# Constants of square roots as numbers, norm scaling on GpSimd, and one add of a block from VectorE to ScalarE

## The chip, the core and the metric

The kernel runs on one core of a Trainium2 chip, all in float32. The core's engines work side by side, each through its own instructions in order: TensorE (PE in the profile, with PEld for its weight loads), VectorE (DVE), ScalarE (ACT), GpSimd (POOL) and SyncE (SP), which here only issues DMAs. They wait for each other through semaphores. The metric is the device time of one execution in microseconds (us), the median of several runs.

## What is computed

Two transformer layers over x of 4 x 1024 x 256. Each layer normalizes, attends, adds, normalizes, applies a feed-forward part and adds. The first layer's attention is a recurrent state (RWKV) and its feed-forward part a mixture of experts; the second layer is the pair attention below with a ternary feed-forward network. The second layer takes three quarters of the time and holds the main part of the change. Cut to it:

```python
def _rho_signed_sqrt(x):
    return jnp.sqrt(jax.nn.relu(x) + EPS_RHO) - jnp.sqrt(jax.nn.relu(-x) + EPS_RHO)
q = jnp.einsum('bnc,ac->bna', X, Wq)                # X: 4 x 1024 x 256, 64 channels a
k = jnp.einsum('bnc,ac->bna', X, Wk)
Vy = jnp.einsum('bnc,dc->bnd', X, Wy_w) + Wy_b
e = jax.nn.relu(_rho_signed_sqrt(q[:, :, None, :] + k[:, None, :, :]))
scores = jnp.einsum('bija,a->bij', e, Wphi)
ex = jnp.exp(scores - jnp.max(scores, axis=-1, keepdims=True))
denom = jnp.sum(ex, axis=-1)
part1 = jnp.einsum('bij,bjc->bic', ex, Vy)
Ew = jnp.einsum('bij,bija->bia', ex, e)
part2 = jnp.einsum('bia,ca->bic', Ew, We_w) + We_b * denom[..., None]
return (part1 + part2) / (denom[..., None] + EPS_DEN)
```

For every pair of a query i and a key j and each of 64 channels, a root of relu(q + k) + eps has to be made: 268 million roots. A layer norm is (x - mean) / sqrt(var + eps), followed by a scale and a shift per channel.

## The kernel before

**The first layer** (`first_layer`) runs over units of 512 tokens. Its roots are in `normed` (L328) and in `outputs` (L516), with eps read from a tile. Its own `normed` scales on DVE (L334) and is not touched otherwise.

**The second layer** (`pair_attention`) works in 128 blocks of 32 queries against 1024 keys. A block has 32 queries x 64 channels x 1024 keys of roots to make. Its queries and channels are spread over the 128 partitions, so that the block consists of 16 operations of 128 x 1024, numbered i = 0 to 15, held in 8 tiles "s" of two each (a pair p has i = 2p and 2p + 1). Each pair goes through this:

- `begin(p)`: for those i which the table ADDS gives to POOL ("p"), POOL adds the query's column to the keys (L1399), then clamps between 0 and the largest number (L1404), over one half or both halves of the tile.
- `adds(p)`: for those that ADDS gives to DVE ("d"), DVE adds and takes the maximum with 0 (L1413).
- `pair(p)`: for those that ADDS gives to ACT ("a"), ACT does a relu with the query as its bias (L1424). Then ACT takes the root of the whole tile of 128 x 2048 (L1425), and PE makes 8 products (16 records in the trace) that sum the scores in `sc` (L1429).
- `weigh(p, h, ew)`: DVE multiplies the tile's half with the exponentials in `xb` and sums (L1475). This frees the tile.

Between them stand, once for a block: `top` (DVE's maximum over the scores, L1439, L1441, and a product on PE, L1442), `exps` (DVE's L1446, then ACT's exponential L1448, and behind it the silu or gelu of the dense part, L1372, through `switch`), `spread` (PE's copy of the exponentials into `xb`, L1455) and `turn`.

The tiles "s" are a ring of 14 (RING). The main loop goes over blocks n and turns p = 0 to 7. In turn p it emits the weighing of pair p of block n, the DVE add of the pair that ACT will take next, at p = 5 `top` and at p = 6 `exps` of the next block, then `work(ROOM[p])`, and then `begin` and `make` of later pairs, 14 ahead for `begin` and two less for `make`. All queues are in the order of emission, written out by hand. Before the change ADDS reads

```python
ADDS = ('ap', 'pp', 'pp', 'dp', 'pp', 'ap', 'dp', 'ap')
```

so that pairs 0, 5 and 7 have their first add on ACT, pairs 3 and 6 on DVE, and the other 11 of 16 are POOL's. In block 0 the rule is another: ACT has i < 6 and DVE the rest.

**Work between the turns.** `work(room)` steps generators. `tasks` holds `finish`, the output of four blocks; `stream` holds the larger parts in order: `first_rest` (the first layer's last unit), `prepare(b)` (queries, keys and values of the next batch, started at block 12 of a batch of 32) and `dense(j)`, the feed-forward network for 256 tokens, of which there are 16, one for each eight blocks. A generator yields the number of its products, until a turn's room is used up; a yield without a number ends the stream's turn. So a turn of PE carries the scores of one pair and up to six dense products.

**The second layer's `normed`** (L917 to L952) is a generator too, called 16 times with n = 2 tiles from `head` (the start of a `dense`), 6 times with n = 4 from `prepare` and once from `first_rest`: 23 calls and 60 tiles of 128 x 256. DVE makes the statistics (L925, L926), ACT the root (L928), DVE after a yield the reciprocal (L930). For two tiles at a time DVE then scales (L937), PE transposes (L941) and, after another yield, ACT applies scale and shift (L944). The scaled tiles `ln_xn` have two buffers.

Of the kernel before, what the change touches and what calls it, by code (L numbers as in the profile page):

```python
# [31 lines left out]
PREP = 12  # L32
ROOM = (4, 6, 6, 6, 6, 4, 3, 6)
LATE = 2
ADDS = ('ap', 'pp', 'pp', 'dp', 'pp', 'ap', 'dp', 'ap')
FIRST_ON_SCALAR = 6
LEAD = 2
FLT_MAX = 3.4028234e38
# [5 lines left out]
@with_exitstack  # L44
def block_kernel(ctx: ExitStack, tc: tile.TileContext, a, out):
    nc = tc.nc
    keep = ctx.enter_context(tc.tile_pool(name="keep", bufs=1))


    kept = ctx.enter_context(tc.tile_pool(name="kept", bufs=1, space=DRAM))  # L50
    link = {
        "x1": [kept.tile([U, C], F32, tag=f"x1_{j}", name=f"x1_{j}") for j in range(B * T // U)],
        "x2": [kept.tile([FB, C], F32, tag=f"x2_{j}", name=f"x2_{j}") for j in range(B * T // FB)],
        "gates": [kept.tile([1, 2, B, C], F32, tag=f"gates{j}", name=f"gates{j}") for j in range(2)],
        "brow": kept.tile([1, C], F32, tag="brow", name="brow"),
        "yg": kept.tile([P, 4, U], F32, tag="yg", name="yg"),
        "qd": kept.tile([T, 64], F32, tag="qd0", name="qd0"),
        "nd": kept.tile([64, T], F32, tag="nd0", name="nd0"),
        "kd": kept.tile([8, P, T], F32, tag="kd0", name="kd0"),
        "vd": kept.tile([T, C + 1], F32, tag="vd0", name="vd0"),  # L60
    }

    ident = keep.tile([P, P], F32, tag="ident", name="ident")
    nc.scalar.dma_start(ident, a["ident"])
    eps = keep.tile([P, 3], F32, tag="eps", name="eps")
    for i, v in enumerate((EPS_LN, EPS_GN, EPS_RHO)):
        nc.vector.memset(eps[:, i : i + 1], v)
    cols = [keep.tile([P, 6, 2, B], F32, tag=f"mcols{i}", name=f"mcols{i}") for i in range(2)]
    seen = keep.tile([P, NE], F32, tag="seen", name="seen")
    link["qt"] = [keep.tile([P, 64, 8], F32, tag=f"qt{i}", name=f"qt{i}") for i in range(2)]  # L70
    link["wsel"] = [keep.tile([P, n], F32, tag=f"wsel{n}", name=f"wsel{n}") for n in (16, 8)]
    nc.gpsimd.memset(seen, 0.0)
    first_layer(tc, a, link, cols, seen, ident, eps)
    pair_attention(tc, a, link, out, cols, seen, ident, eps)


class Router:
# [73 lines left out]
    nc.sync.dma_start(qt[16 * i : 16 * i + 16], qd.rearrange("(m i) n -> i m n", i=16)[:, :, 8 * i : 8 * i + 8])  # L151


def first_layer(tc, a, link, cols_of, seen, ident, eps):

# [13 lines left out]

    nc = tc.nc
    NJ = 2 * HN
    eps_ln, eps_gn = eps[:, 0:1], eps[:, 1:2]
    cols = cols_of[0]
    with tc.tile_pool(name="fl_x", bufs=1) as xp, tc.tile_pool(name="fl_w", bufs=1) as wp, tc.tile_pool(
        name="fl_wd", bufs=2
# [141 lines left out]
        def normed(u, first, dest, cols=cols):  # L319

            b, xu = u * U // T, rows_of_x(u)
            st = p1.tile([P, UT, 6], F32, tag="ln_st", name="ln_st")
            mv = p1.tile([P, UT, 2], F32, tag="ln_mv", name="ln_mv")
            for i in range(UT):
                nc.vector.bn_stats(st[:, i, :], xu[:, i, :])
                nc.vector.bn_aggr(mv[:, i, :], st[:, i, :])
            rs = p1.tile([P, UT], F32, tag="ln_rs", name="ln_rs")
            nc.scalar.activation(rs, mv[:, :, 1], AF.Sqrt, bias=eps_ln)  # L328
            yield
            nc.vector.reciprocal(rs, rs)  # L330

            def scaled(t):
                xn = p2.tile([P, C], F32, tag="ln_xn", name="ln_xn")
                nc.vector.tensor_scalar(xn, xu[:, t, :], mv[:, t, 0:1], rs[:, t : t + 1], ALU.subtract, ALU.mult)  # L334
                return xn

            xs = [scaled(0), scaled(1)]
            yield
            for hf in range(2):
                ps = misc([P, 2, 2 * P], "ln_ps")  # L340
                for i in range(2):
                    xn = xs.pop(0)
                    for cc in range(2):
                        nc.tensor.transpose(ps[:, cc, i * P : (i + 1) * P], xn[:, cc * P : (cc + 1) * P], ident)
                    del xn
                    if not hf:
                        xs.append(scaled(2 + i))
                yield
                for cc in range(2):
                    nc.scalar.activation(  # L350
                        dest[:, cc, 2 * hf * P : 2 * (hf + 1) * P],
                        ps[:, cc, :],
                        AF.Identity,
                        bias=cols[:, first, cc, b : b + 1],
                        scale=cols[:, first + 1, cc, b : b + 1],
                    )
                del ps
# [139 lines left out]
        def outputs(u):  # L497

            while summed.get(u, 0) < 2:
                yield  # L500
            b, xu = u * U // T, rows_of_x(u)
            y, gat = ready[u].pop("v"), ready[u].pop("g")
            ready.pop(u)
            sq = p1.tile([P, 2, U], F32, tag="wide", name="sq")
            for cc in range(2):
                ps = misc([P, U], "cen_ps")
                nc.tensor.matmul(ps, center, y[:, cc, :], start=True, stop=True)
                yield
                nc.scalar.activation(sq[:, cc, :], ps, AF.Square)
                nc.scalar.copy(y[:, cc, :], ps)  # L510
                del ps
            for cc in range(2):
                ps = misc([P, U], "var_ps")
                nc.tensor.matmul(ps, avg, sq[:, cc, :], start=True, stop=True)
                yield
                nc.scalar.activation(sq[:, cc, :], ps, AF.Sqrt, bias=eps_gn)  # L516
                del ps
            for cc in range(2):
                nc.vector.reciprocal(sq[:, cc, :], sq[:, cc, :])
                yield  # L520
                yc, g = y[:, cc, :], gat[:, cc, :]
                nc.vector.scalar_tensor_tensor(yc, yc, chan[:, cc, CH_LW : CH_LW + 1], sq[:, cc, :], ALU.mult, ALU.mult)
                nc.vector.scalar_tensor_tensor(g, yc, chan[:, cc, CH_LB : CH_LB + 1], g, ALU.add, ALU.mult)
            yield
            for t in range(0, UT, 2):
                ps = misc([P, 2, C], "wo_ps")
                for i in range(2):
                    for cc in range(2):
                        nc.tensor.matmul(
                            ps[:, i, :], gat[:, cc, (t + i) * P : (t + i + 1) * P], wm["o"][:, cc, :], start=cc == 0, stop=cc == 1  # L530
                        )
                yield
                tmp = p1.tile([P, 2, C], F32, tag="res", name="res")
                nc.vector.tensor_tensor(tmp, ps, rows[:, 0, b : b + 1, :].to_broadcast([P, 2, C]), ALU.mult)
                del ps
                nc.gpsimd.tensor_add(xu[:, t : t + 2, :], xu[:, t : t + 2, :], tmp)
                del tmp
# [298 lines left out]
        finished(moe)  # L836


def pair_attention(tc, a, link, out, cols_of, seen, ident, eps):

# [7 lines left out]
    nc = tc.nc  # L850
    NB = T // 32
    cols = cols_of[1]
    eps_ln, eps_gn, eps_rho = (eps[:, i : i + 1] for i in range(3))
    src, dst = link["x1"], link["x2"]
    with tc.tile_pool(name="at_k", bufs=1) as pk, tc.tile_pool(name="at_w", bufs=1) as wp, tc.tile_pool(
        name="at_2", bufs=2
# [63 lines left out]
        def normed(xl, n, b, first, hT, cols=cols):  # L920
# [3 lines left out]
            for i in range(n):  # L924
                nc.vector.bn_stats(st[:, i, :], xl[:, i, :])  # L925
                nc.vector.bn_aggr(mv[:, i, :], st[:, i, :])  # L926
            rs = p2.tile([P, n], F32, tag="ln_rs", name="ln_rs")
            nc.scalar.activation(rs, mv[:, :, 1], AF.Sqrt, bias=eps_ln)  # L928
            yield
            nc.vector.reciprocal(rs, rs)  # L930
            for i in range(0, n, 2):
                while not banks[0]:
                    yield
                ps = bank([P, 2, 2 * P], "ln_ps")
                for j in range(2):
                    xn = p2.tile([P, C], F32, tag="ln_xn", name="ln_xn")
                    nc.vector.tensor_scalar(  # L937
                        xn, xl[:, i + j, :], mv[:, i + j, 0:1], rs[:, i + j : i + j + 1], ALU.subtract, ALU.mult
                    )
                    for cc in range(2):  # L940
                        nc.tensor.transpose(ps[:, cc, j * P : (j + 1) * P], xn[:, cc * P : (cc + 1) * P], ident)  # L941
                yield
                for cc in range(2):
                    nc.scalar.activation(  # L944
# [123 lines left out]
        def first_rest():  # L1068
# [37 lines left out]
            for cc in range(2):  # L1106
# [3 lines left out]
                nc.tensor.matmul(ps, avg, flat[:, cc, :], start=True, stop=True)  # L1110
                yield 2
                yield
                nc.scalar.activation(flat[:, cc, :], ps, AF.Sqrt, bias=eps_gn)
                del ps
                banks[0] += 1
            yield
# [261 lines left out]
        class Block:  # L1378
# [38 lines left out]
            def pair(self, p):  # L1417
# [3 lines left out]
                for h in range(2):  # L1421
                    i = 2 * p + h
                    if self.on_scalar(i):
                        nc.scalar.activation(t[:, h, :], kB[self.b][i % 8], AF.Relu, bias=self.query(i))  # L1424
                nc.scalar.activation(t, t, AF.Sqrt, bias=eps_rho)  # L1425
                for h in range(2):
                    g = (2 * p + h) % 8
                    for j in range(4):
# [315 lines left out]
```

## Time and profile before

The time before is 4841.81 us, the median of 3 runs (4838.57 to 4844.68). The profiled execution took 4842.18 us, its span is 4840.4 us; the granted clock of TensorE was 0.916 of full speed on average.

| Line | Engine | Operation | Count | Mean ns |
|---|---|---|---|---|
| L1475 | DVE | weigh half a tile | 2048 | 1212 |
| L1399 | POOL | add, 128 x 1024 | 1397 | 1151 |
| L1404 | POOL | clamp, 128 x 2048 | 381 | 1927 |
| L1404 | POOL | clamp, 128 x 1024 | 635 | 1092 |
| L1429 | PE | score products (records) | 16384 | 412 |
| L1330 | PE | dense products (records) | 4096 | 394 |
| L928 | ACT | root of a norm's variance | 23 | about 300 |

The table is read so: line and engine name a group of like instructions of kernel.py, "mean ns" is one instruction's duration. Matmuls overlap each other, so that their durations can't be added. The profile also tells which work ended each wait ("x <- y: us in total, times, longest us") and a chain of waits: from the last instruction back to what released it, and so on, which gives each line's share of the path that set the end.

### The profile page before, as it was taken

The numbers are of one execution on the slowest core, as the hardware profiler recorded it, in microseconds if no ns is written. First come the engines' busy times: TensorE is split into PE (matmuls) and PEld (weight loads), VectorE is DVE, ScalarE is ACT, GpSimd is POOL, SyncE is SP. The second block draws the span as 40 slices with busy tenths as digits, with TensorE's granted clock in tenths as the row PEclk, the third lists the DMA queues.
The fourth block names the chain that finished last, engine by engine and source line by source line (L and its number), as shares of the span: only waits on it lengthen the run. The fifth ranks groups of instructions, "written<-read, shape, count | busy, mean of one in ns | idle before, by whom it ended". The sixth has DMA issues, their size and how long they took to land.

```text
span 4840.4 us, 76605 instructions
## 1 busy us (share of the span) xinstructions
PE 4247.3 (88%) x28714; PEld 2421.3 (50%) x28714; DVE 3925.3 (81%) x6874; ACT 3411.3 (70%) x3182; POOL 3545.5 (73%) x2882
## 2 busy tenths in 40 slices
PE   6899999986889788989898989888899899898888
PEld 1233333432346455656554655555455556555567
DVE  5899999868897787888887787888877878888871
ACT  2333333228888888888987887888888888988851
POOL 3544444337898788888987888898878988989840
PEclk8799999987899898999998999999899989999899
DMA  4344333441112232312122332212132322122223
GB/s 139 91 119 118 107 111 110 129 137 34 42 62 72 78 98 73 125 56 90 64 73 84 102 110 75 89 64 77 54 112 94 106 72 90 64 75 76 77 85 116
DMA packets 255955, 429.48 MB, mean 89 GB/s; under 512 B 71784, under 2 KB 142624, under 8 KB 255328
## 3 DMA queue, kind: packets, MB, share of 16 engines
q1 hardware_dynamic: 252512, 422.09, 27.7%
q8 instruction: 226, 3.70, 0.3%
q10 hardware_dynamic: 2880, 1.98, 0.1%
q14 instruction: 145, 1.19, 0.1%
q0 software_dynamic: 192, 0.52, 0.0%
HBM read 400.32 MB, written 40.93 MB: 91 GB/s over the span
## 4 chain that ended last, share of the span: by engine, by line
PE 59%; ACT 15%; DVE 13%; issue 7%; POOL 5%; DMA 1%; SPq 0%; ACTq 0%; POOLq 0%; DVEq 0%
PE ff_ps L1330 16%; PE sc L1429 13%; ACT s L1425 7%; PE e_ps L620 7%; DVE s L1475 4%; PE ff_ps L1260 4%; PE xb L1455 3%; POOL s L1399 3%; POOL s L1404 2%; PE out_ps L1351 2%; PE o L1526 2%; DVE state L813 2%; PE proj_ps L425 2%; PE mix_ps L405 1%; ACT s L1424 1%
## 5 line engine op out<-in xcount | busy, mean ns | idle before, releaser
L1475 DVE CUSTOM_DVE_ANT_0 s<-s,xb 128x1024 f32<-128x1024 f32 x2048 | 2394.0, 1212 | 60.5 <-PE xb L1455 48.4
L1425 ACT ACTIVATE s<-s,eps 128x2048 f32<-128x2048 f32 x1024 | 2019.2, 1999 | 125.9 <-POOL s L1404 64.7
L1399 POOL TENSOR_SCALAR s<-kB,qt 128x1024 f32<-128x1024 f32 x1397 | 1599.7, 1151 | 321.7 <-DVE ew L1475 129.7
L1404 POOL TENSOR_SCALAR s<-s 128x1024 f32<-128x1024 f32 x1016 | 1427.4, 1405 | 89.1
L1429 PE MATMUL sc<-s,wsel 128*32 128x256 f32 x16384 | 1170.2, 412 | 329.4 <-ACT s L1425 328.7
L1330 PE MATMUL ff_ps<-wide,fw 128*128 128x256 f32 x4096 | 1001.8, 394 | 24.3 <-ACT wide L1372 21.1
L1429 PEld LDWEIGHTS sc<-s,wsel 128*32 128x32 f32 x16384 | 459.1, 115 | 900.1 <-ACT s L1425 482.2
L1330 PEld LDWEIGHTS ff_ps<-wide,fw 128*128 128x128 f32 x4096 | 762.5, 193 | 231.0 <-issue 102.2
L745 POOL TENSOR_TENSOR kv<-vb,out_k 128x512 f32<-128x512 f32 x256 | 323.7, 1273 | 242.9 <-DVE state L813 163.1
L1424 ACT ACTIVATE s<-kB,qt 128x1024 f32<-128x1024 f32 x387 | 439.5, 1136 | 18.2 <-DVE acc L603 17.5
L620 PE MATMUL e_ps<-wd,hid 128*128 128x512 f32 x896 | 414.6, 609 | 7.0 <-DVE acc L603 4.3
L1455 PE MATMUL xb<-ex,pick 64*128 64x256 f32 x2048 | 317.3, 432 | 46.2 <-ACT ex L1448 45.9
L813 DVE TENSOR_TENSOR_SCAN state<-dec,carry,kv 128x512 f32<-128x512 f32 x256 | 326.1, 1274 | 25.3 <-ACT dec L800 19.6
L620 PEld LDWEIGHTS e_ps<-wd,hid 128*128 128x128 f32 x896 | 169.7, 195 | 231.0 <-issue 216.9
L1413 DVE TENSOR_SCALAR s<-kB,qt 128x1024 f32<-128x1024 f32 x264 | 283.6, 1076 | 0.3 <-issue 0.3
L1455 PEld LDWEIGHTS xb<-ex,pick 64*128 64x128 f32 x2048 | 191.1, 201 | 178.9 <-ACT ex L1448 78.4
L1260 PE MATMUL ff_ps<-wide,fw 128*128 128x256 f32 x1024 | 269.9, 413 | 6.2 <-ACT wide L944 5.8
L805 ACT COPY carry<-state 128x1 f32<-128x1 f32 x255 | 47.9, 188 | 300.3 <-DVE state L813 299.8
L1439 DVE TENSOR_REDUCE sc<-sc 128x1 f32<-128x256 f32 x128 | 55.0, 430 | 243.7 <-PE sc L1429 243.6
L1314 DVE TENSOR_TENSOR wide<-ff_ps,ffn_s 128x512 f32<-128x512 f32 x128 | 87.9, 687 | 195.0 <-PE ff_ps L1330 194.6
L1260 PEld LDWEIGHTS ff_ps<-wide,fw 128*128 128x128 f32 x1024 | 200.3, 205 | 66.2 <-issue 20.6
L1448 ACT ACTIVATE ex<-sc,neg 128x256 f32<-128x256 f32 x128 | 60.7, 474 | 227.0 <-DVE neg L1446 226.3
(254 smaller groups left out, 4168.9 us busy)
## 6 DMA issues: line engine op xcount, KB each, us to landing
fw<-in_ffw_dram SPq DMA_DIRECT2D x354, 512.0 KB
vb<-vd SPq DMA_DIRECT2D x1024, 64.0 KB
lent<-vd SPq DMA_DIRECT2D x64, 514.0 KB
wd<-in_w_down_dram SPq DMA_DIRECT2D x28, 1024.0 KB
kB<-kd SPq DMA_DIRECT2D x32, 512.0 KB
lent<-in_We_dram SPq DMA_DIRECT2D x32, 512.0 KB
kd<-nd SPq DMA_DIRECT2D x24, 512.0 KB
vd<-out_v SPq DMA_DIRECT2D x8, 512.0 KB
```

Source lines behind the costliest of these rows:

```text
L620: nc.tensor.matmul(ps, hid[:, k, t * P : (t + 1) * P], wd[:, k, :], start=k == 0, stop=k == HID // P - 1)
L745: nc.gpsimd.tensor_mul(kv, vb[:, g % 2, :], ready[u]["k"][:, n // HN, :])
L813: nc.vector.tensor_tensor_scan(s[:, 1 : U + 1], dec, kv, c, ALU.mult, ALU.add)
L1260: nc.tensor.matmul(ps[:, h, :], w[:, k, o : o + P], hT[:, k, :], start=k == 0, stop=k == 1)
L1330: nc.tensor.matmul(ps[:, h, :], w[:, k * P : (k + 1) * P], of[:, k, :], start=k == 0, stop=k == 7)
L1399: nc.gpsimd.tensor_scalar(self.s[p][:, h, :], kB[self.b][i % 8], 1.0, self.query(i), ALU.mult, ALU.add)
L1404: nc.gpsimd.tensor_scalar(both, both, FLT_MAX, 0.0, ALU.min, ALU.max)
L1424: nc.scalar.activation(t[:, h, :], kB[self.b][i % 8], AF.Relu, bias=self.query(i))
L1425: nc.scalar.activation(t, t, AF.Sqrt, bias=eps_rho)
L1429: nc.tensor.matmul(self.sc[32 * j : 32 * j + 32, 0:256], wsel[:, g, 16 * (1 - s) : 16 * (1 - s) + 32], t[:, h, 256 * j : 256 * (j + 1)], s ...
L1455: nc.tensor.matmul(xb[:, 256 * j : 256 * (j + 1)], pick[q, j % 2, s, :], self.ex[q, :], start=True, stop=True)
L1475: nc.vector.tensor_tensor_reduce(t[:, h, :], t[:, h, :], self.xb[s], 1.0, 0.0, ALU.mult, ALU.add, ew[:, self.n % 4, col : col + 1])
```

## The change

Three edits. The roots get their eps as a number in the instruction, and the tile of constants goes. The second layer's `normed` flips the sign of the means on DVE, scales on POOL (add, then multiply) before it asks for a bank of PSUM, and yields twice between scaling and transposes. Pair 6 has its first add on ACT in place of DVE. (Parameters `eps` dropped from calls are left out.)

```diff
-ADDS = ('ap', 'pp', 'pp', 'dp', 'pp', 'ap', 'dp', 'ap')
+ADDS = ('ap', 'pp', 'pp', 'dp', 'pp', 'ap', 'ap', 'ap')
...
-    eps = keep.tile([P, 3], F32, tag="eps", name="eps")
-    for i, v in enumerate((EPS_LN, EPS_GN, EPS_RHO)):
-        nc.vector.memset(eps[:, i : i + 1], v)
...
-            nc.scalar.activation(rs, mv[:, :, 1], AF.Sqrt, bias=eps_ln)
+            nc.scalar.activation(rs, mv[:, :, 1], AF.Sqrt, bias=EPS_LN)
...
-                nc.scalar.activation(sq[:, cc, :], ps, AF.Sqrt, bias=eps_gn)
+                nc.scalar.activation(sq[:, cc, :], ps, AF.Sqrt, bias=EPS_GN)
...
                 nc.vector.bn_aggr(mv[:, i, :], st[:, i, :])
+            nc.vector.tensor_scalar_mul(mv[:, :, 0], mv[:, :, 0], -1.0)
             rs = p2.tile([P, n], F32, tag="ln_rs", name="ln_rs")
-            nc.scalar.activation(rs, mv[:, :, 1], AF.Sqrt, bias=eps_ln)
+            nc.scalar.activation(rs, mv[:, :, 1], AF.Sqrt, bias=EPS_LN)
             yield
             nc.vector.reciprocal(rs, rs)
             for i in range(0, n, 2):
+                xs = []
+                for j in range(2):
+                    xn = p2.tile([P, C], F32, tag="ln_xn", name="ln_xn")
+                    nc.gpsimd.tensor_scalar(
+                        xn, xl[:, i + j, :], mv[:, i + j, 0:1], rs[:, i + j : i + j + 1], ALU.add, ALU.mult
+                    )
+                    xs.append(xn)
+                del xn
+                yield
+                yield
                 while not banks[0]:
                     yield
                 ps = bank([P, 2, 2 * P], "ln_ps")
                 for j in range(2):
-                    xn = p2.tile([P, C], F32, tag="ln_xn", name="ln_xn")
-                    nc.vector.tensor_scalar(
-                        xn, xl[:, i + j, :], mv[:, i + j, 0:1], rs[:, i + j : i + j + 1], ALU.subtract, ALU.mult
-                    )
                     for cc in range(2):
-                        nc.tensor.transpose(ps[:, cc, j * P : (j + 1) * P], xn[:, cc * P : (cc + 1) * P], ident)
+                        nc.tensor.transpose(ps[:, cc, j * P : (j + 1) * P], xs[j][:, cc * P : (cc + 1) * P], ident)
+                del xs
                 yield
...
-                nc.scalar.activation(t, t, AF.Sqrt, bias=eps_rho)
+                nc.scalar.activation(t, t, AF.Sqrt, bias=EPS_RHO)
```

## The prediction

> **What bounds the kernel now.** I read the engines' busy times first, then the stretches, the chain of waits, the groups of instructions by line, and last the timeline. The three kinds of work lie one after the other: a first layer until 1102.6 us, the 128 blocks of pair attention until 4697.6 us, and 143 us in which only the last dense products are left. Columns of a stretch: its bounds, its length, then busy us and instructions of PE, PEld, DVE, ACT and POOL; the clock and the DMA come last.
>
> ```profile
> 1102.60:4697.60 3595.00, 3143.19 (x25380) 1923.31 (x25377) 2999.71 (x5406) 3064.70 (x2256) 3064.71 (x2461) 0.91 0.24 79
> 4697.60:4840.40 142.80, 124.25 (x541) 106.31 (x540) 18.58 (x36) 14.46 (x15) 3.25 (x3) 0.94 0.34 113
> 4048.50:4264.50 216.00, 193.00 (x1600) 121.20 (x1596) 183.67 (x331) 190.97 (x139) 193.66 (x156) 0.93 0.23 74
> ```
>
> The third line is one round of eight blocks, which recurs every 216 us. No engine is the bound alone: PE is busy 89% of the round, POOL 90%, ACT 88%, DVE 85%. What a change of 3% in one engine is worth must then be read from the chain of waits over the block stage, with the share that each line has of the path:
>
> ```profile
> by line: PE ff_ps L1330 21.9%; PE sc L1429 17.7%; ACT s L1425 9.6%; DVE s L1475 5.5%; issue 5.5%; PE ff_ps L1260 4.8%; PE xb L1455 4.5%; POOL s L1399 3.7%; POOL s L1404 2.9%; PE out_ps L1351 2.6%; PE o L1526 2.5%; ACT s L1424 1.9%; ACT L142
> ```
>
> PE's named lines alone are 54% of it. What ACT, DVE and POOL gain counts only in the rest, and there they take turns, because they wait for each other in a ring:
>
> ```profile
> PE sc L1429 <- ACT s L1425: 328.7, 204, 8.1
> DVE sc L1439 <- PE sc L1429: 243.6, 79, 10.5
> ACT ex L1448 <- DVE neg L1446: 226.3, 70, 9.2
> POOL s L1399 <- DVE ew L1475: 129.7, 128, 5.1
> ```
>
> PE's score products wait for ACT's root, DVE's maximum (L1439) for the products, ACT's exponential for that maximum, and POOL's next add for a tile that DVE frees.
>
> **The change, part by part.** These groups price it (busy us, mean ns):
>
> ```profile
> L1425 ACT ACTIVATE s<-s,eps 128x2048 f32<-128x2048 f32 x1024 | 2019.2, 1999 | 125.9 <-POOL s L1404 64.7 <-DVE s L1413 22.3 <-ACT s L1424 1.5
> L1372 ACT ACTIVATE wide<-wide 128x2048 f32<-128x2048 f32 x32 | 61.1, 1911 | 67.3 <-DVE wide L1314 66.9
> L1424 ACT ACTIVATE s<-kB,qt 128x1024 f32<-128x1024 f32 x387 | 439.5, 1136 | 18.2 <-DVE acc L603 17.5
> L1413 DVE TENSOR_SCALAR s<-kB,qt 128x1024 f32<-128x1024 f32 x264 | 283.6, 1076 | 0.3 <-issue 0.3
> L937 DVE TENSOR_SCALAR ln_xn<-wide,ln_mv,ln_rs 128x256 f32<-128x256 f32 x28 | 26.6, 988 | 0.5
> L937 DVE TENSOR_SCALAR ln_xn<-res,ln_mv,ln_rs 128x256 f32<-128x256 f32 x32 | 32.1, 1044 | 0.6
> L334 DVE TENSOR_SCALAR ln_xn<-x,ln_mv,ln_rs 128x256 f32<-128x256 f32 x68 | 31.7, 504 | 3.0 <-PE ln_ps L344 2.3
> ```
>
> *Constants.* The roots at L1425 read eps from a tile; the activations at L1372, of the same size, read none and take 88 ns less. 1024 x 0.088 = 90 us off ACT. On the path L1425 has 9.6% of 3595 = 345 us, 173 roots: 173 x 0.088 = -15 us. Ends: 0 (the number is still fetched like a tile) and -90 (every root on the path). I take -15, because the changed program's order of instructions lists the root with its data as sole input and no memset for the constants. The few small roots of the norms and the first layer (44 more) weigh under 4 us and are left at nothing: ACT is idle 70% of the first layer's time.
>
> *Pair 6 from DVE to ACT.* ACT gets 127 adds more (block 0 has its own rule): 127 x 1.136 = +144 us, so that ACT is up 54 us net. The present adds at L1424 have 1.9% of 3595 = 68 us on the path, 15.5% of their 439.5; the new ones at that share: +22 us. Ends: 0 and +144. DVE loses 127 x 1.076 = 137 us. Its main line L1475 has 5.5% of 3595 = 198 us on the path, 8.3% of 2394: -11 us. Ends 0 and -137. The pair's root now waits for no DVE; that wait was only 22.3 us for both pairs.
>
> *Norms.* 60 scalings leave DVE: 26.6 + 32.1 = 59 us. In the stretch of a preparing norm, 2550 to 2600 us, the eight of them took 7.9 us, and of the path in that stretch L937 had 5.6% of 50 us = 2.8 us, 35% of them:
>
> ```profile
> by line: ACT s L1425 15.8%; DMA wide<-x 14.2%; DVE s L1475 13.8%; PE sc L1429 11.5%; PE q_ps L985 7.2%; ACT s L1424 6.3%; DVE ln_xn L937 5.6%; DVE ln_st L925 5.4%; issue 4.2%; ACT wide L944 3.2%; DVE ln_mv L926 2.9%; ACT ewt L1495 2.7%; PE
> ```
>
> So 59 x 0.35 = -21 us; ends 0 and -59. POOL gets 60 of a form that the trace doesn't have there. Below: the clamp L1404 takes 1041 ns for 1024 elements and 1894 for 2048 at their fastest, so 256 would take 0.40 us. Above: the add of two tensors of 128x256 at L1550, 0.734 us. I take 0.55, since two per-partition operands come on top (L1399 with one takes 81 ns more than L1404 at the fastest): 33 us. L1399 and L1404 have 6.6% of 3595 = 237 us on the path, 7.8% of their 3027: +3 us. A sign flip on DVE, 23 x 0.16 us (the small operations at L930), adds 1 us at most. Norms together: -17 us.
>
> *The wait that comes with it.* On POOL the scaling stands in order before the next L1399 and waits for DVE's reciprocal (L930). Behind it queue the adds that ACT's roots need. POOL's adds waited behind that reciprocal already 16.2 us in 9 cases, 1.8 us each. 23 norms x 1.8 = 41 us at the upper end, of which 7.8% on the path, 3 us, if POOL is then as little on the path as now; I take 0, since DVE itself stood at the reciprocal then and the ring held POOL back anyway.
>
> *Collisions.* DVE's one-input operations and POOL's delay each other. Columns: start, us, engine, line.
>
> ```profile
> 3006.71 0.75 DVE L1413 TENSOR_SCALAR s<-kB,qt 128x1024 f32<-128x1024 f32 x1
> 3014.08 1.04 POOL L1404 TENSOR_SCALAR s<-s 128x1024 f32<-128x1024 f32 x1
> 3014.23 1.44 DVE L1413 TENSOR_SCALAR s<-kB,qt 128x1024 f32<-128x1024 f32 x1
> 3015.22 1.44 POOL L1399 TENSOR_SCALAR s<-kB,qt 128x1024 f32<-128x1024 f32 x1
> ```
>
> With POOL idle DVE's add takes 0.75 us; begun during a POOL operation it ends 0.69 us later, and POOL's next takes 1.44 where 1.12 is its floor. Over the floors L1399 and L1404 lose 77 us in all. About half goes with pair 6 and the norms: 38 x 7.8% = -3 us. End: -38.
>
> *Order.* Two added yields per pair of tiles make a norm two turns longer. In the order of PE's instructions the dense products lag by up to 92 of 2816 after a preparation, catch up before each next one, and 30 more (276 for 246) stand behind the last scores. A dense product (two records in the trace) takes 0.466 us there (22.39 us for 96 records): +14 us in the tail, and -14 x 0.59 = -8 in the blocks, by PE's share of the whole run's chain: +6 us. Ends: -8 and +14.
>
> ```profile
> PE 59%; ACT 15%; DVE 13%; issue 7%; POOL 5%; DMA 1%; SPq 0%; ACTq 0%; POOLq 0%; DVEq 0%
> ```
>
> **Sum**: -15 + 22 - 11 - 17 - 3 + 6 = -18 us. The profiled execution took 4842.18 us, of which 4840.4 is the span; the median of the runs is 4841.81, so 4842 serves for both: **4824 us**.
>
> **Two rules that speak against the change.** The Trainium skill (ScalarE: Activation LUTs, Rules for kernel authors) says that adds and relus belong on VectorE. VectorE: DVE Perf Modes (the section on the TRN2 errata) would price DVE's add in its two-fold mode at (58 + 512)/0.96 = 0.59 us, an estimate; 127 of these are worth 75 us and the DVE term 6 instead of 11: 4829. The row says 1.08, and 0.75 undisturbed. The GPSIMD Engine Reference (Engine selection) keeps elementwise work on VectorE. The first layer's L334 shows why, 0.40 us at its fastest; with 60 x 0.40 = 24 us saved at 35% the sum would be 4837. But beside a busy POOL the row is 1.0 us, and I go by the row.
>
> **Rivals.** *ACT becomes the bound* (slower). Pairs 5, 6, 7 and 0 then make ACT do add and root four times in a row between two exponentials, just before DVE's maximum needs pair 7. Its price is the 54 us net; it decides once ACT holds over half of the path outside PE. With 60% of ACT's terms counting (-54 + 86), no DVE gain, norms -10, order and collisions +3: 4867. For it: ACT idles only 25 us of a 216 us round. Against: 226 us of its idle time is one wait, for L1446, after these pairs. *PE holds everything* (no change): every gain outside PE's part is met by a PE wait, and only norms at -10 and order at +6 remain: 4838. For it: PE's 89%. Against: PE waited 328.7 us for roots. *DVE counts for more* than its chain share: POOL's waits for tiles are DVE's lateness, and a ring of four waits shows only its last link. With 30% of 137 + 59 us, ACT's +7, +3: 4793. *POOL's new wait on the path*: +41 us on the forecast, 4865.
>
> **How the numbers follow.** A measurement of this kernel tells about 0.2%, 9.7 us, from no change. Forecast 0.40 and DVE for more 0.12: faster 0.52. PE holds: same 0.18. ACT bound 0.22 and POOL's wait 0.08: slower 0.30. The forecast alone spans 4800 to 4848, from its terms' halves and doubles; for 8 in 10 the range takes in most of the rivals of both signs, 4782 to 4868.
>
> **What would show it.** Roots at 1.91 us; L1413 at half its count and nearer 0.75; no DVE scaling beside POOL, and POOL's at 0.4 to 0.73 us; ACT up by some 54 us, DVE down by 190, POOL within 20; the wait of DVE's maximum for scores no longer than 244 us; the tail 14 us longer. Wrong if ACT's share of the chain grows by more than 3 points, if POOL waits for L930's successor more than 60 us, or if the round of eight blocks is not shorter than 216 us.

## The result, and the profile after

The changed kernel takes 4865.40 us (median of 6 runs, 4861.63 to 4867.41) where the kernel before takes 4839.57 us beside it (6 runs): a ratio of 1.0049, with a 95% interval of 1.0039 to 1.0059. It is slower by 26 us (24 against the median of the time before), where the forecast was 18 us faster. The profiled execution took 4862.24 us, 4860.5 of it the span. The lines of the changed kernel stand three lower: L1425 is now L1428, L1424 is L1427, L1413 is L1416, L1399 is L1402, L1404 is L1407; the norm's scaling is L931.

First the busy times, and then the groups by line (count, busy us, mean ns, idle time ahead of them and what ended it), of the kernel after:

```profile
PE 4258.4 (88%) x28714; PEld 2425.3 (50%) x28714; DVE 3757.6 (77%) x6707; ACT 3455.7 (71%) x3310; POOL 3533.0 (73%) x2942
```

```profile
L1428 ACT ACTIVATE s<-s 128x2048 f32<-128x2048 f32 x1024 | 1925.2, 1907 | 115.0 <-POOL s L1407 52.6 <-DVE s L1416 13.5 <-POOL s L1402 0.7
L1427 ACT ACTIVATE s<-kB,qt 128x1024 f32<-128x1024 f32 x514 | 585.3, 1139 | 18.3 <-DVE acc L599 17.5
L1416 DVE TENSOR_SCALAR s<-kB,qt 128x1024 f32<-128x1024 f32 x137 | 143.3, 1049 | 0.0
L1402 POOL TENSOR_SCALAR s<-kB,qt 128x1024 f32<-128x1024 f32 x1397 | 1582.6, 1139 | 313.8 <-DVE ew L1478 112.5 <-PE sc L1432 60.7 <-DVE neg L1449 34.1
L931 POOL TENSOR_SCALAR ln_xn<-res,ln_mv,ln_rs 128x256 f32<-128x256 f32 x32 | 17.6, 556 | 23.2 <-DVE ln_rs L926 11.2 <-PE sc L1432 10.4 <-issue 1.6
```

Each edit did what the diff says, at the prices foreseen. The root fell from 1999 to 1907 ns. ACT has 127 adds more at 1139 ns, DVE 127 less, and POOL scales a tile in 556 ns. Only DVE's remaining adds got hardly cheaper: 1049 ns after 1076, not nearer 750. So prices of instructions are not where the forecast failed; the waits are:

```profile
PE sc L1432 <- ACT s L1428: 354.9, 219, 7.2
DVE sc L1442 <- PE sc L1432: 313.3, 89, 9.5
DVE wide L1317 <- PE ff_ps L1333: 250.5, 59, 12.2
ACT ex L1451 <- DVE neg L1449: 208.4, 60, 6.5
```

PE waits 26 us longer for roots than before (328.7), although each root is 92 ns shorter. DVE's maximum waits 70 us longer for score products (243.6), and DVE's dense steps wait 56 us longer for PE (194.6 us at L1314 before). Selected lines of the timeline, start and length in us, show the first two at work (in brackets the idle time ahead of an operation and what ended it):

```profile
4411.91 0.43 DVE L1442 TENSOR_REDUCE sc<-sc 128x1 f32<-128x256 f32 x1 [2.27 <-PE sc L1432]
...
4427.92 1.15 ACT L1427 ACTIVATE s<-kB,qt 128x1024 f32<-128x1024 f32 x1
...
4429.16 1.92 ACT L1428 ACTIVATE s<-s 128x2048 f32<-128x2048 f32 x1
4430.99 1.13 ACT L1427 ACTIVATE s<-kB,qt 128x1024 f32<-128x1024 f32 x1
4432.21 1.91 ACT L1428 ACTIVATE s<-s 128x2048 f32<-128x2048 f32 x1
4434.02 1.14 ACT L1427 ACTIVATE s<-kB,qt 128x1024 f32<-128x1024 f32 x1
4434.17 1.07 PE L1432 MATMUL sc<-s,wsel 128*32 128x256 f32 x16 [1.97 <-ACT s L1428]
4435.25 1.91 ACT L1428 ACTIVATE s<-s 128x2048 f32<-128x2048 f32 x1
4436.73 0.43 DVE L1442 TENSOR_REDUCE sc<-sc 128x1 f32<-128x256 f32 x1
4437.21 1.93 PE L1432 MATMUL sc<-s,wsel 128*32 128x256 f32 x16 [1.97 <-ACT s L1428]
```

ACT does add, root, add, root almost without a gap, one pair in about 3.05 us, and PE twice stands 1.97 us idle for a root. DVE's maximum at 4411.91 stood 2.27 us idle for score products. The next one, at 4436.73, didn't wait: DVE was weighing up to it. The chain of waits of this profile can't be used: it breaks off at POOL's scaling with a single unexplained gap.

By stretches, the pair attention starts at 1105.4 us (1102.6 before), and 173.5 us remain behind the last block's maximum (168.7 before). The rest of the loss is inside the blocks. Eight blocks near the end (112 to 119), with the same 1596 weight loads in both, are the clearest; the first line is of before, the second of after (bounds, length, busy us and instructions of PE, PEld, DVE, ACT, POOL):

```profile
4264.50:4480.70 216.20, 191.43 (x1600) 119.98 (x1596) 182.99 (x331) 190.80 (x139) 193.35 (x156) 0.94 0.22 74
```

```profile
4271.90:4495.00 223.10, 196.78 (x1600) 122.13 (x1596) 174.44 (x321) 194.06 (x146) 192.02 (x158) 0.92 0.22 72
```

The same products take 6.9 us longer, and no engine is fuller in share of the time: ACT was busy 88% and is now 87%, POOL 89% and 86%. An engine that had become the bound of these blocks would show the opposite, so that load alone doesn't explain them. PE is busy 5.35 us longer with the same products, at a granted clock of 0.92 for 0.94 (the number third from the end); by an estimate, if all of PE's time goes with the clock, 191.43 x 0.94 / 0.92 - 191.43 = 4.2 us of it come from there.

### The profile page after: what moved, and what is told of

The parts are those of the page before. It is cut to its first block, busy times and chain, and to the rows that moved or that the text cites. A ratio compares the mean times of both kernels' runs of the same rounds, so it can differ in the third digit from the quotient of the medians.

```text
span 4860.5 us, 76632 instructions
## 1 busy us (share of the span) xinstructions
PE 4258.4 (88%) x28714; PEld 2425.3 (50%) x28714; DVE 3757.6 (77%) x6707; ACT 3455.7 (71%) x3310; POOL 3533.0 (73%) x2942
## 5 line engine op out<-in xcount | busy, mean ns | idle before, releaser
L1428 ACT ACTIVATE s<-s 128x2048 f32<-128x2048 f32 x1024 | 1925.2, 1907 | 115.0 <-POOL s L1407 52.6
L1402 POOL TENSOR_SCALAR s<-kB,qt 128x1024 f32<-128x1024 f32 x1397 | 1582.6, 1139 | 313.8 <-DVE ew L1478 112.5
L1407 POOL TENSOR_SCALAR s<-s 128x1024 f32<-128x1024 f32 x1016 | 1400.1, 1378 | 89.0
L1427 ACT ACTIVATE s<-kB,qt 128x1024 f32<-128x1024 f32 x514 | 585.3, 1139 | 18.3 <-DVE acc L599 17.5
L811 DVE TENSOR_TENSOR pr<-state,rec 128x512 f32<-128x512 f32 x256 | 176.0, 688 | 37.6 <-ACT state L807 9.6
```

Source lines behind the costliest of these rows:

```text
L1402: nc.gpsimd.tensor_scalar(self.s[p][:, h, :], kB[self.b][i % 8], 1.0, self.query(i), ALU.mult, ALU.add)
L1407: nc.gpsimd.tensor_scalar(both, both, FLT_MAX, 0.0, ALU.min, ALU.max)
L1428: nc.scalar.activation(t, t, AF.Sqrt, bias=EPS_RHO)
```

## The experiments

All were timed in five rounds beside the kernel before, with 4 to 11 runs of each. The medians of the kernel before were 4841 to 4842 us; ratios are to it, with 95% intervals, and an interval reaches some 4 to 7 us to either side.

**The parts one by one.** In `e1_const` only the roots' constants are numbers; in `e2_adds` only ADDS is changed; in `e3_norm` only the norms, with their two yields.

```diff
 e1_const
-                nc.scalar.activation(t, t, AF.Sqrt, bias=eps_rho)
+                nc.scalar.activation(t, t, AF.Sqrt, bias=EPS_RHO)
 e2_adds
-ADDS = ('ap', 'pp', 'pp', 'dp', 'pp', 'ap', 'dp', 'ap')
+ADDS = ('ap', 'pp', 'pp', 'dp', 'pp', 'ap', 'ap', 'ap')
 e3_norm
-                    nc.vector.tensor_scalar(
...
+                    nc.gpsimd.tensor_scalar(
...
+                yield
+                yield
```

> Only the constants are numbers; ADDS and the norms are as before. Both theories say that this helps: 173 roots on the path by 88 ns, some 4825 us against 4840; L1425's group (another line number here) at 1.91 us. If the time is 4835 or more, ACT's gain of 90 us is met by waits nearly everywhere.

> Only pair 6 goes from DVE to ACT; constants and norms as before. Theory A (ACT: four pairs in a row with add and root hold up the scores): slower by 25 to 50 us, 4865 to 4890, and PE's wait for ACT's roots grows by more than 30 us. Theory B (order: the norm's two yields move the dense products into worse turns): nearly the forecast's two terms, +11 us, 4850 at most.

> Only the norms: sign flip on DVE, scaling on POOL, two yields; constants and ADDS as before. Theory A: faster, 4815 to 4830. Theory B: slower, 4860 or more, with the round of eight blocks (blocks 116 to 123) near 224 us in place of 216.

| Kernel | Median us | Ratio |
|---|---|---|
| e1_const | 4819.65 | 0.9950 [0.9938, 0.9963] |
| e2_adds | 4885.02 | 1.0084 [1.0071, 1.0098] |
| e3_norm | 4856.80 | 1.0028 [1.0017, 1.0040] |

The constants gain 23 us. Both other parts lose: pair 6 on ACT 43 us, the norms 14 us, which the forecast had as a gain. In the sum, -23 + 43 + 14 = +34, against +23 measured (4865 over the 4842 beside these three), so the parts don't merely add. `e2_adds` is in theory A's range; PE's wait for roots grew by 28 us to 357.0, and theory A asked for over 30. `e3_norm` lies between the ranges of both theories, nearer to B.

**Two parts at a time.** `e4_const_adds` has constants and ADDS with the old norms, `e5_const_norm` constants and norms with the old ADDS.

> Constants and pair 6, with the norms as before: the changed kernel without its norms. Theory A: still slower than before, 4850 to 4870. Theory B: faster than before, 4820 to 4835.

> The changed kernel with pair 6 left on DVE (constants and norms changed). If the losses of pair 6 (13.7 us upon the constants) and of the norms just add, 4820 + 14.5 = 4834. If they meet in the same stretches of ACT, the norms cost little here: 4820 to 4828.

`e4_const_adds` took 4833.35 us (0.9985 [0.9976, 0.9994]), `e5_const_norm` 4839.89 us (0.9997 [0.9988, 1.0006]). Pair 6 costs 14 us upon the constants alone and 4865 - 4840 = 25 us upon constants and norms. Upon the shorter root it costs less (43 without), but it never pays. The norms take back nearly all that the constants gain. `e4_const_adds` is in theory B's range by its time; `e5_const_norm` is above both of its expectations.

**What in the norms costs.** The norms are two edits: the engine of the scaling, and two yields for each pair of tiles. `e6_const_norm_no_yields` keeps the first alone, `e7_const_yields_dve` the second alone (scaling on DVE); `e8_change_no_yields` is the whole change without the yields.

```diff
 e6, e8 (against the changed norm)
                 del xn
-                yield
-                yield
                 while not banks[0]:
```

> Constants, and the norms scaled on POOL, but without the two added yields: the transposes come in the turn of the scaling, as before. Theory B1 (the yields move the dense products): the loss goes, 4805 to 4822. Theory B2 (POOL's scaling itself delays the adds behind it): the loss stays, 4830 to 4840, and PE now waits for the scaling as well.

> Constants, and the norms scaled on DVE as before, but early and with the two yields before the transposes: the order of the changed kernel without POOL's work. Theory B1: slower than e1_const's 4820 by 14 us or more, 4834 to 4850. Theory B2: 4815 to 4824.

> The changed kernel without the two yields. Theory B1: the norms' loss upon constants and pair 6 (32 us) goes: 4825 to 4840. Theory B2: 4855 to 4870.

| Kernel | Median us | Ratio |
|---|---|---|
| e6_const_norm_no_yields | 4810.52 | 0.9937 [0.9925, 0.9950] |
| e7_const_yields_dve | 4839.18 | 1.0000 [0.9991, 1.0009] |
| e8_change_no_yields | 4838.26 | 0.9995 [0.9986, 1.0003] |

All three are in the ranges of theory B1, the yields. Scaling on GpSimd gains 9 us (4819.65 to 4810.52); the intervals of e1 and e6 overlap, so that the size of this gain is uncertain. The yields cost 20 us with DVE's scaling (e1 to e7), 29 with POOL's (e6 to e5) and 27 in the whole change (e8 to after). They are about half of what the change gives back (27 of 55 us). The wait of POOL for DVE's reciprocal isn't the loss: e6 has that wait too (15.6 us at L931) and is the fastest kernel of this study. Nor is the granted clock: it was 0.918 in e6's profiled execution and 0.919 in e5's. What the yields are there for, they do: PE stands 20.6 us idle for POOL's scaling in e6 and 3.0 us in e5. They cost more than that elsewhere. e6 also shows what the change could have been: constants and scaling on GpSimd alone beat both kernels.

**Is it the weights that are loaded twice?** The yields bring 361 loads of 512 KB for the dense layers instead of 354, because the next group's head is drawn into the present group's products more often, and then a weight tile that it has used is fetched again.

```diff
 e9_change_no_reloads (against the changed kernel)
-                if k not in held:
+                if k not in held and k not in gone:
...
             held.pop(j * ALL + i)
+            gone.add(j * ALL + i)
```

> The changed kernel with one rule more: a weight tile of the dense layers that has been used isn't loaded a second time (352 loads of 512 KB instead of 361). Order of PE's instructions and yields stay. If the loss from the two yields (27 us on the changed kernel, 4838 without them) comes from the repeated loads, which take one of four weight buffers and let PE wait 10.9 us for weights at L1263: 4838 to 4850, and that wait gone. If it comes from the order, head of the next group drawn into the present one and preparations moved: 4858 to 4866, the wait perhaps shorter.

It took 4867.47 us (1.0053 [1.0040, 1.0065]), with 352 loads. The loads cost nothing that shows. PE's wait for weights in the heads is still there as well, so it doesn't come from them (idle us ahead of the group, behind the second bar):

```profile
L1264 PE MATMUL ff_ps<-wide,fw 128*128 128x256 f32 x1024 | 269.3, 413 | 11.3 <-DMA fw<-in_ffw_dram 10.6 <-ACT wide L947 0.7
```

**Which yields, and how.** `e11_const_norm_one_yield` has one yield for two. `e12_yields_in_head_only` keeps both in the norms of the dense layers' heads, `e13_yields_in_prepare_only` in the norms of the preparations. All have the constants, scaling on GpSimd and the old ADDS.

```diff
 e12 (e13 has "first == 0")
+                if first == 3:
                     yield
                     yield
```

> Constants and norms on GpSimd with one yield instead of two (0: 4810, 2: 4840), old pair adds. 356 loads of weights (0 yields: 354, 2 yields: 361). If each yield costs its turn alike: about 4825. If it is how often a next group's head is drawn into the present group's dense products (2 of 16 with none, 9 with two, 4 with one): about 4818. If the forecast's own order term were right, 3 us per yield: 4813.

> Constants and norms on GpSimd, old pair adds, the two yields only in the norms of the dense layers' heads (16 of the 23 norms), none in the preparations' norms. By PE's order its rounds settle in a pattern of dense products per block of 10, 28, 36, 16, 16, 0, 28, 42 (with no yields: 16, 16, 42, 22, 28, 28, 8, 16), the same 176 in all, and 308 stand behind the last maximum instead of 278. If that uneven order is what the yields cost: 4835 to 4845, its last full round 222 us for 215. If it is only the longer preparations: 4811 to 4818.

> As before, the two yields only in the preparations' norms. By PE's order the uneven pattern follows a preparation for some rounds and then falls back to that of the kernel without yields, 278 products behind the last maximum. If the uneven order costs: 4815 to 4827, between none (4810) and two everywhere (4840), near one yield (4821), the last full round 215 us. If the longer preparations are the cost: 4835 to 4845.

| Kernel | Median us | Ratio | Blocks 112 to 119, us |
|---|---|---|---|
| no yields (e6) | 4810.52 | 0.9937 [0.9925, 0.9950] | 214.9 |
| one (e11) | 4820.95 | 0.9952 [0.9939, 0.9966] | 215.6 |
| two, preparations only (e13) | 4819.84 | 0.9956 [0.9944, 0.9968] | 217.0 |
| two, heads only (e12) | 4845.23 | 1.0008 [0.9999, 1.0016] | 221.9 |
| two, everywhere (e5) | 4839.89 | 0.9997 [0.9988, 1.0006] | 222.1 |

The heads' yields alone cost as much as all of them; those of the preparations cost about 9 us by themselves, as one yield everywhere does (both intervals overlap a little with e6's). e12 and e13 came out about as expected for an uneven order, e12 just above its range of 4835 to 4845, and e13 with a last round 2 us longer than expected; e11 lies between its expectations. What the heads' yields change is the order of PE's work. These are the dense products between one block's maximum and the next in the order of PE's instructions, for the last full round of eight blocks, and below them, from the traces of e6 and e5, all of PE's products (128 score products in each block among them) in blocks 112 to 119 and the block's length in us:

```
order, no yields (e6):       28   28    8   16   16   16   42   22   sum 176
order, two in heads (e12):   10   28   36   16   16    0   28   42   sum 176
e6 products                 181  228  175  180  188  212  213  219   sum 1596
e6 length                  26.9 29.4 23.0 27.0 26.0 27.9 28.9 25.9   sum 214.9
e5 products                 183  217  239  172  188  172  193  232   sum 1596
e5 length                  24.5 30.7 30.2 27.8 25.1 24.4 29.1 30.3   sum 222.1
```

The work is the same, and it lies less evenly: 172 to 239 products in a block for 175 to 228. What that does can be read from the stretches of e5: the whole round, then its most crowded block and the block behind it, one of its two emptiest.

```profile
4251.10:4473.20 222.10, 195.90 (x1600) 121.66 (x1596) 181.16 (x329) 185.20 (x138) 194.60 (x158) 0.92 0.22 72
...
4306.30:4336.60 30.30, 30.30 (x240) 20.65 (x240) 21.82 (x39) 21.41 (x15) 25.31 (x21) 1.00 0.26 87
4336.60:4364.40 27.80, 21.00 (x184) 12.42 (x176) 23.26 (x44) 20.02 (x16) 18.98 (x16) 0.88 0.21 69
```

And the whole round of e6, which has no yields:

```profile
4239.40:4454.30 214.90, 193.38 (x1596) 120.17 (x1596) 180.86 (x330) 185.28 (x139) 195.06 (x158) 0.93 0.22 74
```

DVE, ACT and POOL are busy for the same time in both rounds, within 0.5 us. PE is busy 2.5 us longer, of which the lower granted clock, 0.92 for 0.93, may be 193.38 x 0.93 / 0.92 - 193.38 = 2.1 us by an estimate; that can't be the whole 7.2. In the crowded block PE has no gap at all, at a granted clock of 1.00, and ACT stands for 30.30 - 21.41 = 8.9 us. In the next block PE stands for 27.80 - 21.00 = 6.8 us and ACT and POOL for 7.8 and 8.8: what they couldn't do early is not made up. The reading that fits is that the ring of waits lets no engine run far ahead, so that a round which alternates between PE's limit and the ring's is longer than an even one with the same sum. It is argued, not shown: no run changed the evenness alone, and the number of products doesn't set a block's length by itself (two blocks of e5 with 172 products took 27.8 and 24.4 us).

What is shown is that the order and the longer round go together. All six profiles with two yields in the heads have nearly these products per block and take 220.8 to 223.2 us for blocks 112 to 119; the other ten take 215.0 to 218.6. e12 has the same 1596 products as e6 in four rounds, from blocks 40, 72, 104 and 112: they take 221.8 to 221.9 us in e12 and 214.8 to 215.0 in e6, 28 us in all, and the rest of e12's blocks give back 4. In e5 that holds for the last round alone. Its other rounds have other products than those of e6 and are from 15 us shorter to 12 longer, 12 us longer in all.

**Load or place of pair 6?** `e10_pair3_on_act` is e8 with pair 3 instead of pair 6 on ScalarE: the same counts on each engine. `e14_same_counts_other_pairs` is e6 with pairs 3 and 5 exchanged.

```diff
 e10 (against e8)
-ADDS = ('ap', 'pp', 'pp', 'dp', 'pp', 'ap', 'ap', 'ap')
+ADDS = ('ap', 'pp', 'pp', 'ap', 'pp', 'ap', 'dp', 'ap')
 e14 (against e6)
-ADDS = ('ap', 'pp', 'pp', 'dp', 'pp', 'ap', 'dp', 'ap')
+ADDS = ('ap', 'pp', 'pp', 'ap', 'pp', 'dp', 'dp', 'ap')
```

> Constants and norms without the two yields as in the fastest kernel so far (4810), with pair 3 instead of pair 6 moved from VectorE to ScalarE: as much work leaves DVE and reaches ACT, but pairs 5, 7, 0 and 3 are not four in a row. If ACT's load is what costs: within 5 us of 4838, as with pair 6. If the row of four before the block's maximum costs it: at most 4822. If DVE's relief counts once ACT is not in a row: below 4810.

> Constants and norms without yields (4810), pair adds as many on each engine as before the change, but pair 3 on ScalarE and pair 5 on VectorE instead of the other way round: ScalarE adds in pairs 7, 0 and 3, VectorE in 5 and 6. If it only matters how much each engine does: within 5 us of 4810. If ScalarE's adds cost by standing in a row before the maximum: 4795 to 4806, since only two stand together. If VectorE's two adds just before its maximum cost: above 4815.

`e10_pair3_on_act` took 4820.20 us (0.9956 [0.9944, 0.9969]), `e14_same_counts_other_pairs` 4823.52 us (0.9962 [0.9948, 0.9975]). One more pair on ACT costs 28 us as pair 6 and 10 us as pair 3. So about 18 of the 28 is the place of the moved add, and only the rest can be load. (By the intervals, e10 against e8 is clear; those of e10 and e14 overlap a little with that of e6.) e10 thereby met the second of its expectations, that of the row of four. The wait of DVE's maximum for score products points to the place as well. First e6, then e8, then e10:

```profile
DVE sc L1440 <- PE sc L1430: 262.1, 89, 10.2
```

```profile
DVE sc L1440 <- PE sc L1430: 310.2, 101, 11.0
```

```profile
DVE sc L1440 <- PE sc L1430: 267.4, 88, 11.2
```

Pair 6 adds 48 us to it, pair 3 adds 5. But the row of four stands ahead of every block's maximum, and the difference doesn't fall on every block. These are the stretches from the maximum of block 0 to that of block 40, first e8, then e10:

```profile
1103.30:2238.00 1134.70, 967.04 (x7744) 560.48 (x7748) 897.72 (x1666) 981.89 (x757) 966.81 (x800) 0.90 0.22 72
```

```profile
1105.20:2222.00 1116.80, 952.07 (x7752) 553.58 (x7752) 896.93 (x1666) 981.68 (x757) 965.64 (x800) 0.92 0.23 73
```

Here e8 loses 18 us against e10; over the other 87 blocks it loses 3 (2425.1 against 2421.7), and blocks 112 to 119 take 216.2 us in both. So the row of four can't be the whole account. Two rivals stand untested. PE is busy 15 us longer in e8's 40 blocks at a granted clock of 0.90 for 0.92, and whether the lower clock caused the longer blocks or came with them isn't shown. And DVE keeps another add, that of pair 3 in e8 and that of pair 6 in e10.

The chain of waits, by contrast, would mislead. By engine, e6, e8 and e10:

```profile
PE 60%; DVE 14%; ACT 13%; POOL 7%; issue 3%; DMA 1%; SPq 1%; POOLq 0%; DVEq 0%; ACTq 0%
```

```profile
PE 58%; ACT 17%; DVE 11%; POOL 7%; issue 4%; DMA 1%; SPq 1%; ACTq 0%; POOLq 0%; DVEq 0%
```

```profile
PE 59%; ACT 21%; DVE 11%; POOL 4%; issue 4%; DMA 1%; SPq 1%; ACTq 0%; POOLq 0%; DVEq 0%
```

ACT's share rises by 4 points with pair 6, as a bound on ACT would have it, but by 8 points with pair 3 in a kernel that is 18 us faster. In a ring the share tells whose turn was followed, not what an edit costs. e14 was expected at 4810 if only counts mattered, and at 4795 to 4806 if breaking up ACT's row paid; it was neither. Above 4815 was expected if DVE's two adds just ahead of its maximum cost, and that was met. Exchanging two pairs cost about 13 us without moving any load. Whether that is DVE's two adds side by side in pairs 5 and 6 or ACT's add in pair 3 wasn't separated; the maximum's wait for score products is shorter in e14 than in e6 (232.3 us).

## Why the prediction was wrong

The chain of kernels e1, e6, e8 and after takes the change step by step, so that its differences add to the whole (4842.33 to 4865.40; they are differences of medians from several chips, each uncertain by some us):

| Step | Forecast us | Measured us | Kernels |
|---|---|---|---|
| constants | -15 | -22.7 | before to e1 |
| scaling on GpSimd | -17 | -9.1 | e1 to e6 |
| pair 6 to ScalarE | +22 - 11 = +11 | +27.7 | e6 to e8 |
| collisions | -3 | within the two above | |
| order (the two yields) | +6 | +27.1 | e8 to after |
| sum | -18 | +23.0 | |

**Constants: right mechanism, too small.** 1024 x 0.092 = 94 us went off ACT, and 24% of it reached the end, where the root's chain share gave 17%. The Trainium skill (ScalarE: Activation LUTs, What ACT_TABLE_LOAD costs) has a per-partition operand add about 93 ns to an activation; the row agrees, 1999 - 1907 = 92 ns.

**Norms: right sign, about half the size, as far as two overlapping intervals tell.** The price of POOL's instruction, 0.55 us foreseen, is 0.556. The new wait is there, 11.2 us ahead of the heads' scalings in the row of L931, and 19.9 us with the preparations' included; it was set at 0 on the path, and e6's gain says that little of it is on the path. That rival falls.

**Pair 6: the first step that failed**, "the new ones at that share: +22". The share of the present adds, 15.5%, is a mean over pairs 5, 7 and 0. The new add does not cost what the mean of its like does: +27.7 us as pair 6, 9.7 as pair 3, where the +11 would have been right. As pair 6 it adds 48 us to the maximum's wait for products. Why it costs so much more there, and most of that in the first 40 blocks, stays open. The rival *ACT becomes the bound* named this row of four pairs, and its 4867 is next to the measured 4865. It is not confirmed by that. Its condition, over half of the path outside PE on ACT, doesn't hold in e8 (17 of 42 points) and does in e10 (21 of 41), where the same load costs 10 us; so the 54 us of load from which it was priced don't set the loss. It is also not the whole loss: without the yields the change is at 4838.

**Order: the step that failed worst**, "+14 us in the tail, and -14 x 0.59 = -8 in the blocks: +6". It priced the products that end up behind the last scores. The 30 dense products more came (308 for 278 behind the last maximum), but the tail grew by only 173.5 - 168.7 = 5 us. What the yields cost is inside the blocks, where the forecast had a gain: 22 of the 29 us between the profiled executions of e8 and after lie between the first and the last maximum, and where the products are the same, a round is 7 us longer. That the less even placing of the products does it is the reading that fits. The changed pattern per block was to be seen in PE's order beforehand, and was read for its sum alone.

**One reading of the profile was too simple.** The round does not recur every 216 us: of the 15 full rounds before the change five take 216.0 to 216.3 us from maximum to maximum, the other ten 222.9 to 240.2. A price per round can't be multiplied by 16.

**Collisions.** POOL's adds and clamps did get shorter: L1399 and L1404 took 1599.7 + 734.3 + 693.1 us before and 1582.6 + 731.8 + 668.3 after, 44 us less in all, about as foreseen (38). DVE's own adds stayed at 1049 ns. No run isolates what it was worth.

**What was to show it.** Of the three signs set down for a wrong forecast one came: the round of eight blocks is not shorter (223.1 for 216.2 us). POOL's wait at the scaling stayed under 60 us (19.9), and the chain of the changed kernel can't be read. Of the signs for a right one, the maximum's wait failed (313 us, and not below 244), the tail (5 us longer, not 14) and the price of DVE's adds.

Still open: whether the evenness of PE's work by itself makes the rounds longer; why the yields cost 20 us with DVE's scaling and 27 to 29 with POOL's; what makes pair 6 dear in the first 40 blocks, and how the part that isn't its place divides between ACT's load and the rest; and what in e14 costs.

## What to carry to other kernels

When a change adds or removes a turn in a hand-written interleaving, compare how much work lies in each block before and after, not only how much is left at the end: in this kernel the same products in another, less even order came with 7 us more in a round of 215. Price a moved instruction by the place in which it will stand: the same add cost 28 us as pair 6 and 10 as pair 3, and the mean path share of its like can't tell these apart. Split an edit that carries a scheduling change from the arithmetic that it is meant to make cheaper: here the cheaper arithmetic won 32 us in two parts, and two yields and a moved pair gave back 55.

## What was not expected of the hardware

An elementwise instruction with two per-partition operands on 128x256 took GpSimd 556 ns in the mean (552 to 559 over 32 instructions with POOL's queue as it is after the change; 573 in e6), where DVE took 951 for the same in e7, beside a busy POOL, and 497 for it in e7's first layer. So for this form beside a busy POOL, POOL itself was the faster engine. And DVE's remaining adds stayed at 1049 ns (1076 before) when half of them and its scalings were gone, so these weren't what held them up.
